# An RWKV attention and mixture-of-experts layer on one core: the first block in halves, products in front of three waits, two of the last rows ahead of the branch, one more bank at the end

## The chip, the cores and the metric

The kernel runs on 1 core of a Trainium2 chip. A core has a tensor engine (PE, with its weight loads shown apart as PEld), VectorE (DVE), ScalarE (ACT), GpSimd (POOL) and SyncE (SP), each with an instruction queue of its own that runs in order, and 16 DMA engines that all queues share. Matmul results land in PSUM, which has 8 banks of 128 x 512 float32 words. The metric is the device time of one execution in microseconds (us). Times below are us unless another unit is given.

## The reference

With x of shape (1, 2048, 512), all in float32:

```python
xn = layernorm(x)                                    # over the 512 columns, no weights
# attention: RWKV
r, v, k = split(xn @ W_rvk.T, 3)
# per column c, over the tokens t, with w = -exp(time_decay), u = time_first:
#   y  = (exp(o - no) * p + exp(u + kt - no) * vt) / (exp(o - no) * q + exp(u + kt - no))
#   o, p, q  <-  the running maximum and the two sums scaled to it
attn = (sigmoid(r) * y) @ W_out.T
# experts: 12, of which 8 are real and 4 pass x through; top 2 by softmax + bias
probs = softmax(xn @ classifier_w.T);  idx = top_k(probs + bias, 2);  rw = probs[idx] * 1.5
ffn = sum over the chosen real experts of rw * (silu(xn @ gate_e.T) * (xn @ up_e.T)) @ down_e.T
    + xn * (sum of rw over the chosen pass-through experts)
return x + attn + ffn
```

## The kernel before, in words

The 2048 tokens are four blocks b of 512, and a block is four rows j (row i = 4b + j) of 128 tokens. Everything is written in one hand-set order (`manual_schedule`): each engine runs its instructions in the order in which the Python code issues them.

**Head.** `load_x` and `load_w` put the loads on SP's queue. `norm(b)` (L207) takes the mean and variance of the block's four rows on DVE, then one chain for all four: sd on ACT (L218), seven small DVE instructions to rstd and shift, and the scaling of the rows, on DVE for even j (L232) and on ACT for odd j (L234). `turn_block(b)` (L237) transposes the block on PE, 4 columns c of 4 pieces, into four PSUM banks, each copied out by ACT (L246). The loop at L520 norms the next block while it turns this one, with classifier matmuls (`logits`, `add_quarters`, into the tile pl) and first products in between.

**Products.** `all_products` (L415) is a generator over all matmuls of k, v and r, 176 steps of two matmuls of 512 columns in four-byte floats (PE records each as two passes). k and v of a pair of blocks are made with seven products instead of eight (p1 to p7). Several share a bank: p6 writes a bank py, DVE adds it away; p7 adds into the same bank, DVE adds again (L368); p4 adds into it, DVE adds again (L385). So p7's first matmul waits for p6's add, and p4's first matmul for p7's add. Likewise p3 follows p5 in a bank pz. `fill(n)` issues the next n steps.

**Routing.** From pl, DVE chooses the two experts of each token (L547 to L648), and sorts tokens into 25 tiles of 128 places by expert: for m = 0 and 1 it makes the matrices lowhot and tok (L674 to L692), and PE multiplies them into pi (L695). Between the two, PE gets `fill(5)` (L698).

**Main part.** Sixteen scans (one for each block b and column c, `scan`, L460) run on DVE and ACT in five stages S1 to S5: S1 scans the running maximum, S2 takes exponentials on ACT, S3 scans the two sums, S4 forms the denominator and numerator, S5 divides (a reciprocal of 3.3 us) into yT. Twenty-five expert tiles run beside them. `first_half(i)` (L850) multiplies the tile with its experts' gate and up weights (`up`, L795, four matmuls into pg), applies the activation and asks for the weights of tile i + 2; `second_half(i)` (L866) packs the next tiles (`unite(i + 1)` makes xgT on ACT, L783; `flip(i + 2)`) and finishes tile i - 2 (`finish`, L833: the down product po, yo on ACT, and a scatter by POOL that adds it to the output in DRAM).

A plan sets the order: `plan(at, what)` puts a piece of work at a place in a table that is then sorted by that place. The product steps that are left stand at 0, `one`, 2 `one`, ..., the stages of the scans at fixed places, and the halves of tile i at `4 + spread * i` and `4 + spread * (i + 0.6)`. With 57 of the 176 steps issued before the table, 119 are left, and `one` is (259.86 - 8) / 151 = 1.668 and `spread` is (259.86 - 12) / 25 = 9.914:

```python
    total = (len(left) + CC * len(ROWS)) * ONE + TILES * 5.2
    one = (total - 8) / (len(left) + CC * len(ROWS))
    spread = (total - 12) / TILES
```

**Tail.** Rows of blocks 0 and 1 are multiplied with W_out during the main part (`attention_row`, L973). The rows of block 2 come after the table (`attention`, L905, in turn with the last stages of the last scan), each added to xn times its pass-through weight on DVE (L934). Then a branch (L1038) skips a loop that would run if the tokens needed more than 25 tiles; here it is never entered. After it, SP reads the output rows of block 3 back (`read_out`, which must wait for the last scatter), DVE adds the pass-through part (L901), POOL adds eight finished rows to the output in DRAM (`add_row`, L967, accumulating DMAs), and the four rows of block 3 are multiplied, added (L930) and written (L931), the last one in two halves in one bank.

PSUM is four pools of two banks: mm, gu, o and tr. A new tile takes the bank of its pool that was given back first, and its first writer waits until that bank's last reader is done.

Of the kernel before, what the change touches and what calls it, by code (L numbers as in the profile page):

```python
# [26 lines left out]
F32 = mybir.dt.float32  # L27
# [8 lines left out]
P = 128  # L36
T = 2048
C = 512
CC = C // P
TB = 512  # L40
NTB = T // TB
NJ = TB // P
# [9 lines left out]
TILES = 25  # L52
# [7 lines left out]
def layer(ctx: ExitStack, tc: tile.TileContext, x, w_rvk, w_out, decay, first, cls, ebias, gu, down, out):  # L60
    nc = tc.nc
# [6 lines left out]
    place = pool("place", 1)  # L68
# [6 lines left out]
    small = pool("small", 2)  # L75
# [128 lines left out]
    xnT = {}  # L204
    pl = ps_o.tile([P, NT, ET], F32, tag="o", name="pl")

    def norm(b):  # L207
        js = slice(b * NJ, (b + 1) * NJ)
        for j in range(NJ):
            i = b * NJ + j  # L210
            st = small.tile([P, 6], F32, tag="st", name=f"st{i}")
            nc.vector.bn_stats(st, xt[i])  # L212
            nc.vector.bn_aggr(mv[:, i, :], st)
        var = mv[:, js, 1]
        ve = small.tile([P, NJ], F32, tag="ve", name=f"ve{b}")
        nc.vector.tensor_scalar_add(ve, var, EPS)
        sd = small.tile([P, NJ], F32, tag="sd", name=f"sd{b}")
        nc.scalar.activation(sd, var, AF.Sqrt, bias=eps_sb[:, 0:1])  # L218
        r0 = small.tile([P, NJ], F32, tag="r0", name=f"r0{b}")
        nc.vector.reciprocal(r0, sd)  # L220

        sq = small.tile([P, NJ], F32, tag="sq", name=f"sq{b}")
        nc.vector.tensor_mul(sq, r0, r0)
        nc.vector.tensor_mul(sq, sq, ve)
        nc.vector.tensor_scalar(sq, sq, -0.5, 1.5, ALU.mult, ALU.add)
        nc.vector.tensor_mul(rstd[:, js], r0, sq)
        nc.vector.scalar_tensor_tensor(shift[:, js], mv[:, js, 0], -1.0, rstd[:, js], ALU.mult, ALU.mult)
        for j in range(NJ):
            i = b * NJ + j
            t, r = xt[i], rstd[:, i : i + 1]  # L230
            if j % 2 == 0:
                nc.vector.tensor_scalar(t, t, mv[:, i, 0:1], r, ALU.subtract, ALU.mult)  # L232
            else:
                nc.scalar.activation(t, t, AF.Identity, bias=shift[:, i : i + 1], scale=r)  # L234
        store_xn(b)

    def turn_block(b):  # L237
        xnT[b] = place.tile([P, CC, TB], F32, tag=f"s{2 + b}", name=f"xnT{b}")
        for c in range(CC):
            if c % 2 == 0:  # L240
                pt = ps_tr.tile([P, TB], F32, tag="tr", name=f"pt{b}_{c}")
            else:
                pt = ps_gu.tile([P, TB], F32, tag="gu", name=f"pt{b}_{c}")
            for j in range(NJ):
                nc.tensor.transpose(pt[:, j * P : (j + 1) * P], xt[b * NJ + j][:, c * P : (c + 1) * P], ident)
            nc.scalar.copy(xnT[b][:, c, :], pt)  # L246

    lgs = {}

# [205 lines left out]
    def fill(n):  # L455
        for _ in range(n):
            next(products)
        done[0] += n
# [52 lines left out]
    def whole(gen):  # L511
        for _ in gen:
            pass
# [1 line left out]

    manual = ExitStack()
    manual.enter_context(tc.manual_schedule())
    norm(0)
    turn_block(0)
    for b in range(NTB):  # L520
        if b + 1 < NTB:
            norm(b + 1)
# [149 lines left out]
    for m in range(2):  # L672
        ks = slice(m * NT, (m + 1) * NT)
        nc.vector.tensor_tensor(  # L674
            lowhot[:, ks, :],
            lane.unsqueeze(1).to_broadcast([P, NT, P]),
            low[:, m].unsqueeze(2).to_broadcast([P, NT, P]),
            ALU.is_equal,
        )
        nc.vector.tensor_tensor(  # L680
            hh,
            tiles128.unsqueeze(1).to_broadcast([P, NT, MAX_TILES]),
            high_b[:, m].unsqueeze(2).to_broadcast([P, NT, MAX_TILES]),
            ALU.is_equal,
        )
        tok = place.tile([P, NT, NV, MAX_TILES], BF16, tag=f"s{7 + m}", name=f"tok{m}")
        nc.vector.tensor_tensor(  # L687
            tok,
            hh.unsqueeze(2).to_broadcast([P, NT, NV, MAX_TILES]),
            vals[:, m].unsqueeze(3).to_broadcast([P, NT, NV, MAX_TILES]),  # L690
            ALU.mult,
        )  # L692
        for j in range(NT):
            k = m * NT + j
            nc.tensor.matmul(pi, lowhot[:, k, :], tok[:, j], start=(k == 0), stop=(k == NK - 1))  # L695
        if m == 0:
            which_i = place_tiles()
            fill(5)  # L698
    nc.vector.tensor_scalar_mul(wdec, wdec, -1.0)
    cfac = const.tile([P, CC], F32, tag="cfac", name="cfac")  # L700
    nc.vector.tensor_add(cfac, first_sb, wdec)
# [192 lines left out]
    def read_out(b):  # L894

        t = place.tile([P, NJ, C], F32, tag="s0", name=f"orows{b}")
        for j in range(NJ):
# [4 lines left out]
                orows[i], xrows[i], zw[:, i : i + 1], orows[i], ALU.mult, ALU.add  # L902
            )

    def attention(b, js=range(NJ)):  # L905

        for j in js:
            i = b * NJ + j
            if b < NTB - 2:
                po = ps_tr.tile([P, C], F32, tag="tr", name=f"pw{i}")  # L910
            elif j >= 2 if i in orows else j % 2 == 1:
                po = ps_mm.tile([P, C], F32, tag="mm", name=f"pw{i}")
            else:
                po = ps_o.tile([P, C], F32, tag="o", name=f"pw{i}")

            halves = 2 if i == NT - 1 else 1
            n = C // halves
            for h in range(halves):
                hs = slice(h * n, (h + 1) * n)
                for c in range(CC):  # L920
                    nc.tensor.matmul(  # L921
                        po[:, hs],
                        yT[b][:, j, c, :],
                        wout_sb[:, c, hs],
                        start=(c == 0),
                        stop=(c == CC - 1),
                    )
                    yield
                if i in orows:
                    nc.vector.tensor_add(orows[i][:, hs], orows[i][:, hs], po[:, hs])  # L930
                    nc.sync.dma_start(out[i * P : (i + 1) * P, hs], orows[i][:, hs])  # L931
            if i in orows:
                continue
            nc.vector.scalar_tensor_tensor(xrows[i], xrows[i], zw[:, i : i + 1], po, ALU.mult, ALU.add)  # L934

# [57 lines left out]
    def plan(at, what, *args):  # L993
        table.append((at, iter([(what, *args)]) if args else what))
# [108 lines left out]
```

## Time and profile before

| What | us |
|---|---|
| Time, median of 3 runs | 379.12 (378.87 to 379.74) |
| The profiled execution, time | 379.29 |
| The profiled execution, span | 377.5 |
| PE busy | 358.2 |
| DVE busy | 308.9 |
| ACT busy | 161.5 |
| POOL busy | 91.4 |
| First matmul starts | 10.37 |
| Last matmul ends | 374.15 |
| DMA moved | 88.80 MB, mean 235 GB/s |

A line of a timeline starts with the start and the duration of a group of instructions, then engine, source line, operation, tiles written <- tiles read and their shapes; brackets at the end give how long the engine stood idle before it and what ended that. A line of the waits reads: engine, tile, line <- who was waited for: us in total, times, longest. A line for a stretch gives its start and end, its length, and then the busy us (and number of instructions) of PE, PEld, DVE, ACT and POOL, the granted clock of PE, the busy share of the DMA engines and their GB/s. The busy share of the DMA engines can pass 1, since a packet's time holds time that it waits.

### The profile page before, as it was taken

To read this page: it belongs to the slowest core of one execution; us is meant where nothing else is said; L and a number is where in the kernel's file an instruction comes from. 1 tells how busy PE (TensorE), PEld (TensorE's weight loads), DVE (VectorE), ACT (ScalarE), POOL (GpSimd) and SP (SyncE) were. 2 spreads that over 40 slices of the span, in tenths; PEclk is the share of its full clock that TensorE was granted. 3 is DMA by queue.
4 is the path that set the end of the run, shared out by engine and by line. 5 is a ranking of instruction groups with operands and counts; after the bars stand their busy time and mean duration, and the time that the engine had idled before them with its cause. 6 is when DMAs were issued, how large, how long until landed. Compare 5 with 4: busy or idle time off the path is not lost.

```text
span 377.5 us, 3504 instructions
## 1 busy us (share of the span) xinstructions
PE 358.2 (95%) x970; PEld 164.9 (44%) x970; DVE 308.9 (82%) x450; ACT 161.5 (43%) x274; POOL 91.4 (24%) x118
## 2 busy tenths in 40 slices
PE   0899998999999999999999999999999999999995
PEld 0565444543444444444444444444444444444343
DVE  4879899989997997987987779597769786959951
ACT  1677311232653554554556453636354555423000
POOL 5000300210203233322232224133144321102450
PEclk9999999999999999999999999999999999999999
DMA  7998944643657898889898998999999999767497
GB/s 268 399 356 322 334 141 162 227 91 132 177 126 220 257 264 250 251 230 260 220 262 237 272 265 222 271 233 319 258 280 277 290 264 248 195 188 166 93 191 191
DMA packets 63029, 88.80 MB, mean 235 GB/s; under 512 B 42208, under 2 KB 42592, under 8 KB 59232
## 3 DMA queue, kind: packets, MB, share of 16 engines
q1 hardware_dynamic: 55472, 67.85, 61.5%
q0 software_dynamic: 7536, 20.71, 23.5%
q8 instruction: 8, 0.13, 0.1%
q14 instruction: 13, 0.11, 0.1%
HBM read 63.78 MB, written 19.40 MB: 220 GB/s over the span
## 4 chain that ended last, share of the span: by engine, by line
PE 73%; DVE 17%; DMA 5%; ACT 2%; issue 2%; SPq 0%; DVEq 0%
PE pg L795 22%; PE po L836 10%; PE pr L408 9%; PE py L325 9%; PE pw L973 7%; PE pz L325 6%; PE px L325 4%; PE pw L921 4%; DMA x<-in_x_dram 3%; DVE den L505 3%; DMA wrvk<-in_w_rvk_dram 2%; DVE tok L687 2%; DVE sums L490 1%; DVE obv L477 1%; DVE st L212 1%
## 5 line engine op out<-in xcount | busy, mean ns | idle before, releaser
L795 PE MATMUL pg<-gw,xgT 128*128 128x512 f32 x200 | 90.2, 593 | 1.5 <-ACT xgT L783 1.5
L841 POOL DMA_INDIRECT out_dram<-yo,to_i x25 | 45.7, 1826 | 165.0 <-ACT yo L840 114.5
L408 PE MATMUL pr<-xnT,wrvk 128*128 128x512 f32 x128 | 60.6, 593 | 0.0
L795 PEld LDWEIGHTS pg<-gw,xgT 128*128 128x128 f32 x200 | 37.8, 190 | 49.3 <-issue 45.7
L505 DVE RECIPROCAL den<-den 128x512 f32<-128x512 f32 x16 | 53.5, 3345 | 0.0
L836 PE MATMUL po<-dw,actT 128*128 128x512 f32 x100 | 46.9, 593 | 0.5 <-ACT actT L814 0.5
L803 ACT ACTIVATE th<-pg 128x256 f32<-128x256 f32 x25 | 9.6, 384 | 85.0 <-PE pg L795 85.0
L733 POOL DMA_INDIRECT xg<-xs,token_i x25 | 27.0, 1080 | 61.9 <-ACT xp L775 28.3
L408 PEld LDWEIGHTS pr<-xnT,wrvk 128*128 128x128 f32 x128 | 24.1, 190 | 29.2 <-issue 29.2
L804 DVE SCALAR_TENSOR_TENSOR th<-th,pg 128x256 f32<-128x256 f32 x25 | 10.5, 419 | 32.1 <-ACT th L803 32.0
L325 PE MATMUL px<-xnT,wrvk 128*128 128x512 f32 x64 | 32.3, 604 | 0.0
L325 PE MATMUL py<-t,wrvk 128*128 128x512 f32 x64 | 30.7, 594 | 0.0
L783 ACT COPY xgT<-xq 128x1024 uint16<-128x1024 uint16 x25 | 28.9, 1156 | 3.9 <-DMA xq<-xp 3.8
L921 PE MATMUL pw<-wout_sb,yT 128*128 128x512 f32 (+1 forms) x72 | 28.2, 548 | 2.0 <-DVE xrows L934 1.5
L973 PE MATMUL pw<-wout_sb,yT 128*128 128x512 f32 x64 | 30.1, 592 | 0.0
L836 PEld LDWEIGHTS po<-dw,actT 128*128 128x128 f32 x100 | 18.9, 190 | 24.2 <-issue 22.7
L775 ACT COPY xp<-xg 128x1024 uint16<-128x1024 uint16 x25 | 26.1, 1044 | 5.6 <-DMA xq<-xp 4.5
L840 ACT ACTIVATE yo<-po,wplace 128x512 f32<-128x512 f32 x25 | 17.2, 686 | 23.2 <-PE po L836 23.0
L490 DVE TENSOR_TENSOR_SCAN sums<-obv,state,a 128x512 f32<-128x512 f32 x16 | 20.5, 1282 | 4.1 <-ACT obv L483 4.0
L492 DVE TENSOR_TENSOR_SCAN sums<-obv,state,a 128x512 f32<-128x512 f32 x16 | 20.5, 1284 | 0.6
L921 PEld LDWEIGHTS pw<-wout_sb,yT 128*128 128x128 f32 x72 | 13.5, 190 | 17.0 <-issue 13.4
L477 DVE TENSOR_TENSOR_SCAN obv<-wdec,state,k 128x512 f32<-128x512 f32 x16 | 20.5, 1280 | 0.0
(171 smaller groups left out, 459.0 us busy)
## 6 DMA issues: line engine op xcount, KB each, us to landing
gw<-in_gu_dram SPq DMA_DIRECT2D x25, 1024.0 KB, 5.5
dw<-in_down_dram SPq DMA_DIRECT2D x25, 512.0 KB, 5.9
x<-in_x_dram SPq DMA_DIRECT2D x16, 256.0 KB, 5.3
xs<-x SPq DMA_DIRECT2D x16, 256.0 KB, 4.9
wrvk<-in_w_rvk_dram SPq DMA_DIRECT2D x3, 1024.0 KB, 7.2
xrow<-xs SPq DMA_DIRECT2D x8, 256.0 KB, 7.0
xrows<-xs SPq DMA_DIRECT2D x8, 256.0 KB, 5.2
wout_sb<-in_w_out_dram SPq DMA_DIRECT2D x1, 1024.0 KB, 10.6
```

The source lines that it names most:

```text
L325: nc.tensor.matmul(ps, a[:, k, c * P : (c + 1) * P], x[:, k], start=(start and k == 0), stop=(k == 1), skip_group_check=True,)
L408: nc.tensor.matmul(ps, wrvk_sb[0][:, k, c * P : (c + 1) * P], xnT[b][:, k, :], start=(k == 0), stop=(k == CC - 1))
L477: nc.vector.tensor_tensor_scan(o2, w.to_broadcast([P, TB]), k, s[:, 0:1], ALU.add, ALU.max)
L505: nc.vector.reciprocal(den, den)
L733: nc.gpsimd.indirect_dma_start(out=xg, out_offset=None, in_=xs, in_offset=bass.IndirectOffsetOnAxis(ap=token[:, i : i + 1], axis=0),)
L775: nc.scalar.copy(xp, st[i]["xg"].bitcast(U16).rearrange("p (c h) -> p h c", h=2))
L783: nc.scalar.copy(xgT.bitcast(U16).rearrange("p c (t h) -> p c t h", h=2), st[i]["xq"].rearrange("p (h c) t -> p c t h", h=2),)
L795: nc.tensor.matmul(pg, st[i]["xgT"][:, c, :], st[i]["w"][:, c, :], start=(c == 0), stop=(c == CC - 1))
L836: nc.tensor.matmul(po, st[i]["actT"][:, c, :], st[i]["d"][:, c, :], start=(c == 0), stop=(c == IC - 1))
L841: nc.gpsimd.indirect_dma_start(out=out, out_offset=bass.IndirectOffsetOnAxis(ap=to[:, i : i + 1], axis=0), in_=yo, in_offset=None, compute ...
L921: nc.tensor.matmul(po[:, hs], yT[b][:, j, c, :], wout_sb[:, c, hs], start=(c == 0), stop=(c == CC - 1),)
L973: nc.tensor.matmul(po, yT[b][:, j, c, :], wout_sb[:, c, :], start=(c == 0), stop=(c == CC - 1))
```

## The change

Block 0 is normalised and turned in two halves of two rows: `norm` and `turn_block` take a `part`, and the copies out of PSUM, the stores of xn and the tile xnT come with the second half. `fill(5)` between the two products of the routing becomes `fill(6)`, so that 58 steps are issued before the table and 118 are left. `first_half(1)` stands two places later in the plan. The first matmul of the first row of block 2 is put into the plan right ahead of `finish` of the last tile. The rows of blocks 2 and 3 take their banks from the pools o, tr, mm and o in pairs, and the second half of the last row takes a bank of tr. Rows 12 and 13 are multiplied ahead of the branch; their sums and stores follow behind it (`add_rows`), as those of rows 14 and 15 do.

```diff
-    def norm(b):
-        js = slice(b * NJ, (b + 1) * NJ)
-        for j in range(NJ):
+    def norm(b, part=range(NJ)):
+        n = len(part)
+        js = slice(b * NJ + part[0], b * NJ + part[0] + n)
+        for j in part:
...
-        store_xn(b)
-
-    def turn_block(b):
-        xnT[b] = place.tile([P, CC, TB], F32, tag=f"s{2 + b}", name=f"xnT{b}")
+        if part[-1] == NJ - 1:
+            store_xn(b)
+
+    pts = {}
+
+    def turn_block(b, part=range(NJ)):
         for c in range(CC):
-            if c % 2 == 0:
+            if part[0] > 0:
+                pt = pts[c]
+            elif c % 2 == 0:
                 pt = ps_tr.tile([P, TB], F32, tag="tr", name=f"pt{b}_{c}")
             else:
                 pt = ps_gu.tile([P, TB], F32, tag="gu", name=f"pt{b}_{c}")
-            for j in range(NJ):
+            pts[c] = pt
+            for j in part:
                 nc.tensor.transpose(pt[:, j * P : (j + 1) * P], xt[b * NJ + j][:, c * P : (c + 1) * P], ident)
-            nc.scalar.copy(xnT[b][:, c, :], pt)
+            if part[-1] == NJ - 1:
+                if c == 0:
+                    xnT[b] = place.tile([P, CC, TB], F32, tag=f"s{2 + b}", name=f"xnT{b}")
+                nc.scalar.copy(xnT[b][:, c, :], pt)
...
-    norm(0)
-    turn_block(0)
+
+    for part in (range(0, NJ // 2), range(NJ // 2, NJ)):
+        norm(0, part)
+        turn_block(0, part)
...
-            fill(5)
+            fill(6)
...
+    whole_rows = []
+
+    def add_rows():
+
+        for i, hs, po in whole_rows:
+            nc.vector.tensor_add(orows[i][:, hs], orows[i][:, hs], po[:, hs])
+            nc.sync.dma_start(out[i * P : (i + 1) * P, hs], orows[i][:, hs])
+        whole_rows.clear()
+
     def attention(b, js=range(NJ)):
-
         for j in js:
             i = b * NJ + j
-            if b < NTB - 2:
-                po = ps_tr.tile([P, C], F32, tag="tr", name=f"pw{i}")
-            elif j >= 2 if i in orows else j % 2 == 1:
-                po = ps_mm.tile([P, C], F32, tag="mm", name=f"pw{i}")
-            else:
-                po = ps_o.tile([P, C], F32, tag="o", name=f"pw{i}")
+
+            pool_, tag = ((ps_o, "o"), (ps_tr, "tr"), (ps_mm, "mm"), (ps_o, "o"))[(i - (NTB - 2) * NJ) // 2]
+            po = pool_.tile([P, C], F32, tag=tag, name=f"pw{i}")
...
+                if h == 1:
+                    po = ps_tr.tile([P, C], F32, tag="tr", name=f"pw{i}_{h}")
...
-                if i in orows:
-                    nc.vector.tensor_add(orows[i][:, hs], orows[i][:, hs], po[:, hs])
-                    nc.sync.dma_start(out[i * P : (i + 1) * P, hs], orows[i][:, hs])
-            if i in orows:
+                if b == NTB - 1:
+                    whole_rows.append((i, hs, po))
+                    yield
+            if b == NTB - 1:
                 continue
...
-        plan(4 + spread * i, first_half, i, TILES)
+
+        plan(4 + spread * i + (2 if i == 1 else 0), first_half, i, TILES)
         plan(4 + spread * (i + 0.6), second_half, i, TILES)
...
+    third = [attention(NTB - 2, [j]) for j in range(NJ)]
+    plan(6.9 + spread * TILES, third[0])
...
     for j, stops in enumerate((1, 2, 0, 0)):
-        whole(attention(NTB - 2, [j]))
+        whole(third[j])
         for _ in range(stops):
             next(stages[-1])
+    whole(attention(NTB - 1, range(0, 2)))
...
-    whole(attention(NTB - 1))
+    add_rows()
+    for _ in attention(NTB - 1, range(2, NJ)):
+        add_rows()
```

More of the change, by code (lines that the diff above doesn't have):

```diff
@@ L214, in norm @@
         var = mv[:, js, 1]
-        ve = small.tile([P, NJ], F32, tag="ve", name=f"ve{b}")
+        ve = small.tile([P, NJ], F32, tag="ve", name=f"ve{b}_{part[0]}")[:, :n]
         nc.vector.tensor_scalar_add(ve, var, EPS)
-        sd = small.tile([P, NJ], F32, tag="sd", name=f"sd{b}")
+        sd = small.tile([P, NJ], F32, tag="sd", name=f"sd{b}_{part[0]}")[:, :n]
         nc.scalar.activation(sd, var, AF.Sqrt, bias=eps_sb[:, 0:1])
-        r0 = small.tile([P, NJ], F32, tag="r0", name=f"r0{b}")
+        r0 = small.tile([P, NJ], F32, tag="r0", name=f"r0{b}_{part[0]}")[:, :n]
         nc.vector.reciprocal(r0, sd)
-        sq = small.tile([P, NJ], F32, tag="sq", name=f"sq{b}")
+        sq = small.tile([P, NJ], F32, tag="sq", name=f"sq{b}_{part[0]}")[:, :n]
         nc.vector.tensor_mul(sq, r0, r0)
@@ L243, in turn_block @@
                 pt = ps_gu.tile([P, TB], F32, tag="gu", name=f"pt{b}_{c}")
-            for j in range(NJ):
+            pts[c] = pt
+            for j in part:
                 nc.tensor.transpose(pt[:, j * P : (j + 1) * P], xt[b * NJ + j][:, c * P : (c + 1) * P], ident)
-            nc.scalar.copy(xnT[b][:, c, :], pt)
+            if part[-1] == NJ - 1:
+                if c == 0:
+                    xnT[b] = place.tile([P, CC, TB], F32, tag=f"s{2 + b}", name=f"xnT{b}")
+                nc.scalar.copy(xnT[b][:, c, :], pt)
     lgs = {}
```

## The prediction

> **What bounds the kernel now.** I read the page first, then the waits of the tensor engine (PE), then the timeline at the three places where PE waits, and last the stretches of the end.
>
> The busy times and what PE waited for:
>
> ```profile
> PE 358.2 (95%) x970; PEld 164.9 (44%) x970; DVE 308.9 (82%) x450; ACT 161.5 (43%) x274; POOL 91.4 (24%) x118
> ```
> ```profile
> PE pt L245 <- DVE x L232: 10.4, 1, 10.4
> PE pg L795 <- ACT xgT L783: 1.5, 1, 1.5
> PE pw L921 <- DVE xrows L934: 1.5, 1, 1.5
> PE pi L695 <- DVE tok L687: 1.4, 1, 1.4
> PE po L836 <- ACT actT L814: 0.5, 1, 0.5
> PE pw L921 <- DVE orows L930: 0.5, 1, 0.5
> ...
> PEld py L325 <- DVE v L368: 1.2, 2, 0.9
> ```
>
> PE is the bound; its idle time lies in six places, and the change goes at each. The last line (all engines' waits) is the one to remember: a weight load that waited for VectorE (DVE) to read a product out of its bank.
>
> The head, in the timeline:
>
> ```profile
> 7.31 0.69 DVE L212 BATCH_NORM_STATS2 st<-x 128x6 f32<-128x512 f32 x1 [1.12 <-DMA x<-in_x_dram]
> 10.37 3.91 PE L245 MATMUL pt<-ident,x 128*128 128x128 f32 x16 [10.37 <-DVE x L232]
> 14.11 1.88 PE L325 MATMUL px<-xnT,wrvk 128*128 128x512 f32 x4
> 14.79 0.30 ACT L218 ACTIVATE sd<-mv,eps_sb 128x4 f32<-128x4 f32 x1
> 19.60 1.91 PE L245 MATMUL pt<-ident,x 128*128 128x128 f32 x16
> ```
>
> DVE sits idle for the fourth row of x while two rows could already be normalised. The middle, on DVE, PE and the weight loads, and one stretch of 21.9 us:
>
> ```profile
> 101.17 3.34 DVE L505 RECIPROCAL den<-den 128x512 f32<-128x512 f32 x1
> 105.16 0.68 DVE L368 TENSOR_TENSOR v<-v,py 128x512 f32<-128x512 f32 x1
> 108.41 0.68 DVE L368 TENSOR_TENSOR v<-v,py 128x512 f32<-128x512 f32 x1
> ```
> ```profile
> 103.81 3.60 PE L795 MATMUL pg<-gw,xgT 128*128 128x512 f32 x8
> 107.24 3.03 PE L325 MATMUL py<-t,wrvk 128*128 128x512 f32 x6
> ```
> ```profile
> 109.15 0.30 PEld L325 LDWEIGHTS py<-t,wrvk 128*128 128x128 f32 x2 [0.85 <-DVE v L368]
> ```
> ```profile
> 83.30:105.20 21.90, 20.36 (x48) 8.77 (x48) 21.61 (x26) 7.83 (x13) 2.66 (x2) 1.00 0.58 154
> ```
>
> In that stretch (PE, weight loads, DVE, ScalarE (ACT), POOL) DVE is busy 21.61 of 21.90: there DVE, not PE, has no slack. The end, with the DMA share and GB/s in the last columns:
>
> ```profile
> 364.00:369.00 5.00, 5.00 (x13) 2.19 (x12) 2.48 (x4) 0.00 (x0) 0.86 (x1) 1.00 1.12 204
> 369.00:374.00 5.00, 4.49 (x19) 3.05 (x17) 1.11 (x2) 0.00 (x0) 0.00 (x0) 1.00 1.08 276
> 374.00:375.00 1.00, 0.16 (x1) 0.00 (x0) 0.42 (x1) 0.00 (x0) 0.00 (x0) 1.00 0.27 89
> 375.00:376.10 1.10, 0.00 (x0) 0.00 (x0) 0.00 (x0) 0.00 (x0) 0.00 (x0) 1.00 0.39 134
> ```
>
> The DMA engines are full from 358 to 374 (eight accumulating rows of POOL's queue, then output rows) and only the last 2 us have room. The chain of waits names PE there; behind PE stands a second bound just as late.
>
> **Head: block 0 in halves.** The second row's statistics end at 5.09. What takes from 8.26 to 9.68 on DVE (variance to scaling, 1.42) now runs from 5.13, the first two rows are scaled by 7.1 (DVE) and 7.4 (ACT, 0.76). The seven extra small DVE instructions (0.16 to 0.18 each) fall where DVE waited for the fourth row. Rows three and four: statistics 7.0 to 8.7, scaled by 10.7 and 11.1, against 10.68 and 11.31 before; DVE starts block 1 at 10.7, as before (10.66). PE turns 8 of 16 pieces from 7.1 to 9, the other 8 from 11.1 at 0.2 us each, done near 12.6 instead of 14.1. ACT's four copies end near 13.7 instead of 14.9, so block 1's sd leaves at 14.0 (its variances are ready at 13.95) instead of 14.79: block 1 is scaled, and the copy of the first product behind it on ACT leaves, 0.8 earlier. PE needs that copy for p2 (weight load at 18.37, waiting for ACT v). So 1.5 on PE becomes about 0.85, and everything up to the routing (DVE reads pl at 37.84 after a wait of 0.32 for PE) moves by it. Ends: 1.0, set by ACT's copy; and a loss of 0.3 if the products from 12.6 run at half pace until 16.3.
>
> Why half pace: the transposes before 14.0 take 0.20 each (13 weight loads in 2.63), those at 19.6 take 0.12, and the four products at 14.11 come every 0.43, the full pace of the whole kernel. So PE sped up about 3.6 us after it began. I let it speed up at 14.0 again; four products from 12.65 are then done at 15.1, still ahead of ACT's copy at 17.6. [...]
>
> **Middle: fill(6), and first_half(1) two units later.** One product step (two matmuls at 0.43, 0.86) goes into the wait of 1.35 for tok; DVE sets the end of that wait, so what is saved is the 0.86 later. But every product now runs one place earlier against DVE's stages. Walking the queues with the rows' durations, from 66.27 - 0.85 = 65.42:
> - p7 of column 0 now meets the deferred adds and p4 of column 0 meets p7's add, both still on DVE: waits of 0.15 and 0.43. So DVE's add for p5 of column 1 (83.32, which waited 0.19 for PE) comes 0.86 - 0.58 = 0.28 earlier beside the 0.85.
> - The plan now puts seven product steps between tiles 0 and 1, not six. PE reaches tile 1 at 93.58 - 0.85 + 0.58 + 0.86 = 94.17; ACT's xgT, behind DVE's chain, is ready at 95.07 - 0.85 - 0.28 = 93.94. The wait of 1.54 is gone, with 0.2 to spare.
> - Next in line: p4 of column 2 adds into the bank that p7's add reads (DVE, 105.16). Before, the plan held it at 25.02, behind tile 2 (23.83): PE did 3.43 us of pg first. One slot is now (259.0 - 8)/150 = 1.673, p4 is slot 14 at 23.43, and tile 2 stands at 23.76: p4 goes in front. PE arrives at 94.17 + 3.43 + 4 x 0.86 = 101.0. DVE has the same 21.6 us of work before that add, so it ends at 105.84 - 0.85 - 0.28 = 104.7: a new wait of 3.7.
> - The old wait of 0.27 for the second such add (108.41; load at 109.15) goes.
>
> With first_half(1) go ACT's packing copy for tile 0, SyncE's load of tile 3's weights (5.5 to land, wanted some 15 later) and POOL's gather for tile 4 (4.5, likewise); I cost them at nothing for that cover, and at most at the 0.9 by which they leave later.
>
> Sum on PE up to the last tile, from which DVE's last chain hangs (it waited 4.18 for that tile): -0.85 - 0.86 - 1.54 - 0.27 + 0.58 + 3.7 = +0.76. Later waits I expect none: PE idled 0.03 us from 96 to 332, and xgT for tiles 3 and 4 is ready 4 us early. Bounds of the new wait: nothing, if DVE keeps up, and 4.3, if DVE gains only the 0.85 less 0.3.
>
> **End.** The row matmul in front of finish (0.86) covers the wait of 0.52 for actT; it changes POOL's scatters by nothing, since each waits some 5.6 for the one before (345.08, 350.65, then 356.23). The first products of row 12 and the bank wait (1.5, 0.5) go: the last yT ends at 358.64, and 13 row matmuls of 0.86 follow instead of 16 from 359.36. PE ends at 369.9 instead of 374.15: 4.3 earlier, beside the +0.76. A branch between rows 13 and 14 costs PE little: before, PE's semaphore write behind it followed its last matmul by 0.04; at most the 1.5 that PE stood idle there, under the 4.3. DVE, four row sums held by reads that land until 363.8, adds rows 12 and 13 at 365.2, before 365.11 and 366.53; SyncE's five writes leave between 365.6 and 370.4 instead of 374.6. But they wait for DMA engines: a write issued at 365.82 took 6.6 to land, as accumulations filled them (204 GB/s alone). Bytes are the same, so only the idle part goes: 0.73 of 374 to 375 and 0.67 of 375 to 376.1, 1.4 in all. The last accumulation (issued 364.18, 10.6 to land) lands at 374.8 and the program ended 1.2 after its last landing: 1.5 is the most. I take 1.15, nearer to the idle rows, as the last packets spread unevenly; least 0.4, should the last half row (1.7 to land) still come alone.
>
> Sum: +0.76 - 1.15 = -0.4 on a span of 377.5; with 1.79 around it (379.29) 378.9, and with the median 0.17 lower, 378.7.
>
> **Rivals.**
> - The new wait at p4 is not there (DVE keeps up, or the order falls otherwise). For it: before, it cost 0.85 only. Against: the 21.61 of 21.90. Then -3.5 + 0.58 = -2.9, and -1.15: 375.1.
> - Slower: PE stays at half pace from 12.65 to 16.3. Place: the four products and the eight logits matmuls; price 1.8, so that block 1's transposes come at 19.9 instead of 18.75. It decides from about 15.5 on. Then the head loses 0.3, and +1.9 - 1.15 = +0.75: 379.9 to 380.3. For it: PE now pauses from 9 to 10.7. Against: 14.11 came at full pace after 3.7 us.
> - The earlier output rows slow the accumulations and the end gains nothing: +0.76, 379.9. Against: mixed, the engines moved 276 GB/s, alone 204.
> - No change at all to be seen is part of the main case: under 0.2% (0.76 us, about what a measurement of this kernel can tell).
>
> **How the numbers follow.** Main case 0.48, 378.7 with an own range of 377.4 to 379.9; no new wait 0.18; half pace 0.17; no gain at the end 0.10; the rest 0.07. Faster by over 0.2%: a third of the main case, the first rival, some of the rest: 0.37. Slower: a fifth of the main case, half of each of the two others and some rest: 0.26. Same 0.37. The range leaves out half of the first rival and the far end of the slow ones: 375.2 to 380.3.
>
> **What would show it.** Products from about 12.6 and block 1 turned near 18.8; the wait for tok 0.5, none for xgT; a wait of 3 to 4 us of PE for DVE's L368 add near 101 to 105; no waits at actT, xrows, orows; PE done 4 us before the end, and DMA engines full until the last microsecond. Wrong if PE passes p4 without waiting (375), or if products near 13 come every 0.86 for over 3 us.

## The result, and the profile after

| What | before | after |
|---|---|---|
| Median of all executions, us | 379.13 (378.50 to 383.66, 20) | 383.50 (379.75 to 388.69, 20) |
| Ratio, 95% interval | | 1.0085 (1.0060 to 1.0111) |
| Profiled execution, time / span, us | 379.29 / 377.5 | 380.86 / 379.0 |
| Start of the last tile's second half of pg | 331.78 | 333.14 |
| Last matmul ends | 374.15 | 372.55 |
| Last scatter of POOL leaves | 350.65 | 352.08 |

The change makes the kernel slower by 0.85%, 3.2 us. The ratio leaves out four executions of the changed kernel that took over 1.5% more than its fastest (386.02 to 388.69); with them the medians lie 1.15%, 4.4 us, apart. I had forecast 378.7, and 380.3 at the most. The profiled execution is among the quickest of the changed kernel and shows only 1.5 us of the loss in its span; the other half has to be looked for in the executions that it does not show.

The busy times and the waits of the tensor engine (PE), from the page and the view of waits, of the changed kernel (waited for, us in total, times, longest):

```profile
PE 359.4 (95%) x970; PEld 165.2 (44%) x970; DVE 309.9 (82%) x457; ACT 162.0 (43%) x275; POOL 90.9 (24%) x118
```
```profile
PE pt L251 <- DVE x L233: 8.6, 2, 7.2
PE py L334 <- DVE v L377: 3.7, 2, 3.6
PE pi L706 <- DVE tok L698: 0.5, 1, 0.5
```

Of the six idle places before, those at xgT, actT, xrows and orows are gone, tok has shrunk from 1.4 to 0.5, and one of 3.6 us has come: PE waits for a VectorE (DVE) add that reads the bank which p4 of column 2 writes next.

The head, in the timeline (start, duration, then the group):

```profile
7.17 2.06 PE L251 MATMUL pt<-ident,x 128*128 128x128 f32 x8 [7.17 <-DVE x L233]
10.67 2.15 PE L251 MATMUL pt<-ident,x 128*128 128x128 f32 x8 [1.44 <-DVE x L233]
12.60 2.88 PE L334 MATMUL px<-xnT,wrvk 128*128 128x512 f32 x4
...
19.09 1.91 PE L251 MATMUL pt<-ident,x 128*128 128x128 f32 x16
```

The first products start 1.5 us earlier (12.60 for 14.11) but take 2.88 instead of 1.88, as PE reaches its full pace only at 14.61. Block 1 is turned 0.51 earlier.

The middle, on PE and then on DVE:

```profile
94.42 3.70 PE L806 MATMUL pg<-gw,xgT 128*128 128x512 f32 x8
97.96 3.60 PE L334 MATMUL py<-t,wrvk 128*128 128x512 f32 x8
105.13 1.13 PE L334 MATMUL py<-t,wrvk 128*128 128x512 f32 x2 [3.57 <-DVE v L377]
106.09 3.60 PE L806 MATMUL pg<-gw,xgT 128*128 128x512 f32 x8
109.52 2.74 PE L334 MATMUL py<-t,wrvk 128*128 128x512 f32 x6
```
```profile
100.40 3.35 DVE L514 RECIPROCAL den<-den 128x512 f32<-128x512 f32 x1
103.78 0.69 DVE L515 TENSOR_TENSOR yT<-num,den 128x512 f32<-128x512 f32 x1
104.39 1.28 DVE L377 TENSOR_TENSOR v<-v,py 128x512 f32<-128x512 f32 x2
```

p4 stands in front of tile 2, and PE has nothing else that it may do in the meantime. Tile 2, which started at 103.81 before, starts at 106.09.

The end, in stretches (busy time of PE, weight loads, DVE, ScalarE (ACT) and POOL, then the granted clock, the DMA share and GB/s):

```profile
366.00:371.00 5.00, 5.00 (x18) 3.09 (x17) 2.86 (x6) 0.00 (x0) 0.69 (x1) 1.00 1.14 205
371.00:376.00 5.00, 1.56 (x8) 1.02 (x6) 0.71 (x2) 0.00 (x0) 0.00 (x0) 1.00 0.99 276
376.00:377.00 1.00, 0.00 (x0) 0.00 (x0) 0.00 (x0) 0.00 (x0) 0.00 (x0) 0.71 0.19 61
```

PE ends 1.6 us earlier than before, and the program 1.5 later: 6.4 us pass between PE's last matmul and the end, where before it was 3.4. The accumulating rows go at 205 GB/s with the DMA share at 1.14, as before (204 at 1.12).

### The profile page after: what moved, and what is told of

It reads as the page before. It is cut to its first block, busy times and chain, and to the rows that moved or that the text cites. A ratio compares the mean times of both kernels' runs of the same rounds, so it can differ in the third digit from the quotient of the medians.

```text
span 379.0 us, 3515 instructions
## 1 busy us (share of the span) xinstructions
PE 359.4 (95%) x970; PEld 165.2 (44%) x970; DVE 309.9 (82%) x457; ACT 162.0 (43%) x275; POOL 90.9 (24%) x118
## 5 line engine op out<-in xcount | busy, mean ns | idle before, releaser
L939 PE MATMUL pw<-wout_sb,yT 128*128 128x512 f32 (+1 forms) x72 | 28.1, 546 | 0.1
L334 PEld LDWEIGHTS py<-t,wrvk 128*128 128x128 f32 x64 | 11.9, 190 | 20.0 <-issue 12.9
```

What stands on the lines that cost most here:

```text
L334: nc.tensor.matmul(ps, a[:, k, c * P : (c + 1) * P], x[:, k], start=(start and k == 0), stop=(k == 1), skip_group_check=True,)
L939: nc.tensor.matmul(po[:, hs], yT[b][:, j, c, :], wout_sb[:, c, hs], start=(c == 0), stop=(c == CC - 1),)
```

## The experiments

Three theories were put against each other. A: the pause of 3.57 us costs its length and, besides, the granted clock of PE, in most executions. B: the split of block 0 disturbs the clock. C: the end hangs on the DMA engines, so that what PE gives there is lost. The clock of each execution below is the mean granted clock over its span. Where PE ends well before the program, half pace in the last idle microseconds takes 0.002 to 0.005 off it at no cost (0.998 in the first profile with the head whole, 0.995 in that of the rows added early; in the changed kernel's first profile it begins at 376.42, 3.9 behind PE's last matmul, and the clock is 0.997), so that 0.995 to 0.998 can be an execution with no loss.

**Tile 2 ahead of p4 again.**

```diff
-        plan(4 + spread * i + (2 if i == 1 else 0), first_half, i, TILES)
+        plan(4 + spread * i + (2 if i == 1 else -0.5 if i == 2 else 0), first_half, i, TILES)
```

> The changed kernel, with the first half of tile 2 planned 0.5 units earlier (23.26), so that p4 of column 2 (23.43) stands behind it again, as in the kernel before; nothing else is different. Theory A (PE's pause of 3.57 us in front of that p4 is the loss, and it is also what lets PE's clock fall to half for some us in most executions): the wait at line 334 near 105 is gone, the last tile's matmuls end near 330.4 instead of 333.14, the granted clock is 0.997 or more in nearly every execution, and the median is near 377.5, 1.6 under the kernel before. Theory B (the split of block 0 disturbs the clock, the pause costs only itself): the wait is gone too, but most executions still show clocks of 0.98 to 0.99, and the median is near 380.5. Theory C (the end is bound by the DMA engines whatever PE does): PE ends some 9 us before the span does, and the median is no lower than 378.5.

Measured: 377.83, ratio 0.9945 (0.9911 to 0.9979), clocks 0.997 and above in 10 of 12, 0.995 in two. Of the pause 0.2 us is left. The waits and the head of its profiled execution:

```profile
PE pt L251 <- DVE x L233: 8.7, 2, 7.3
PE pi L706 <- DVE tok L698: 0.5, 1, 0.5
PE py L334 <- DVE v L377: 0.2, 1, 0.2
```
```profile
12.73 3.62 PE L334 MATMUL px<-xnT,wrvk 128*128 128x512 f32 x4
...
20.31 1.91 PE L251 MATMUL pt<-ident,x 128*128 128x128 f32 x16
```

One number in the plan turns a loss of 3.2 us into a gain of 2.1. Theory A holds. B falls as far as it needs the split alone, since the split is in here. But the head came out badly in this execution: PE got its full pace at 17.04, so the four products took 3.62 and block 1 was turned at 20.31, later than the 19.60 of the kernel before. That is the half pace that I had as a rival.

**Block 0 in one piece, the rest as changed.**

```diff
-    for part in (range(0, NJ // 2), range(NJ // 2, NJ)):
+    for part in (range(NJ),):
```

> The changed kernel with block 0 normalised and turned in one piece, as before; middle and end as changed. Theory A: the pause in front of p4 of column 2 stays at about 3.6 us, the clocks of the executions stay spread from 0.98 to 1.0, the work to the last tile ends 0.5 later (333.6 against 333.14), and the median is near 384. Theory B (the early transposes and the stop between the halves disturb the clock): every execution has a clock of 0.998 or more, and the median is near 381.2, which is the profiled 380.86 with the 0.5 of the head taken back.

Measured: 382.99, ratio 1.0096 (1.0064 to 1.0128), clocks from 0.987 to 0.998. The loss stays without the split. B falls.

**The split alone**, in the kernel before.

```diff
-    norm(0)
-    turn_block(0)
+    for part in (range(0, NJ // 2), range(NJ // 2, NJ)):
+        norm(0, part)
+        turn_block(0, part)
```

> The kernel before, with block 0 in halves and nothing else. Block 1's transposes on PE come near 19.1 instead of 19.6. My prediction's step gave the head 0.85 and the trace of the changed kernel shows 0.50; how much of it reaches the last tile depends on DVE, which has no slack from 83 to 105: theory A: the median is between 378.4 and 379.2, with clocks as steady as those of the kernel before. Theory B: the clocks spread from 0.98 to 1.0, and the median is 381 to 382.

Measured: 379.55, ratio 1.0005 (0.9975 to 1.0035), clocks 0.998 to 1.0. The split doesn't harm the clock, and no gain shows, though the interval would hide one of 0.5. Why the earlier turn of block 1 (18.82 here, 19.60 before) is not seen in the median is told further down.

**The end alone**, in the kernel before (the banks and `add_rows` of the change are in as well and are not shown again).

```diff
+    third = [attention(NTB - 2, [j]) for j in range(NJ)]
+    plan(6.9 + spread * TILES, third[0])
...
+    whole(attention(NTB - 1, range(0, 2)))
...
-    whole(attention(NTB - 1))
+    add_rows()
+    for _ in attention(NTB - 1, range(2, NJ)):
+        add_rows()
```

> The kernel before, with the end of the change alone: the first row matmul ahead of the last finish, two rows of block 3 ahead of the branch, one bank more. My prediction's step: PE ends near 370 instead of 374.15, the whole program 1.15 earlier, median 378.0. Theory C (accumulations and output rows share the DMA engines and these are full either way, so that what PE gives is lost): PE ends near 370, the last landing stays within 0.4 of 376.0, and the median is 378.9 to 379.5.

Measured: 378.75, ratio 0.9985 (0.9963 to 1.0008). The interval leaves both open; the profile tells them apart: PE ended at 371.24 (374.15 before), the last output packet at 374.97 (376.00), the span was 376.5. That speaks against C, which had it within 0.4 of 376.00: the end gained 1.0 of my 1.15 in that execution, 0.3 of it already at the last scatter (350.36 for 350.65). The last stretch, which idled before at shares of 0.27 and 0.39, is half full:

```profile
368.50:373.50 5.00, 2.73 (x13) 2.08 (x11) 0.85 (x3) 0.00 (x0) 0.00 (x0) 1.00 1.09 270
373.50:375.00 1.50, 0.00 (x0) 0.00 (x0) 0.00 (x0) 0.00 (x0) 0.00 (x0) 1.00 0.57 205
```

**The middle alone**, in the kernel before.

```diff
-            fill(5)
+            fill(6)
...
-        plan(4 + spread * i, first_half, i, TILES)
+        plan(4 + spread * i + (2 if i == 1 else 0), first_half, i, TILES)
```

> The kernel before, with fill(6) and the later first_half(1) alone. Theory A: TensorE pauses 3.6 us in front of p4 of column 2; the last tile's second half of pg starts at 333.6 (331.78 before); clocks spread from 0.985 to 1.0; the median is 382.5 to 384, all of the loss of the changed kernel. If the loss needed the three parts together (the head's stop or the earlier output rows adding to it): the median is 381.0 or less, the 1.8 of the wait alone, with clocks of 0.999 to 1.0.

Measured: 383.61, ratio 1.0118 (1.0072 to 1.0164), and this time the profiled execution has what the medians had only hinted at:

```profile
105.20 1.33 PE L334 MATMUL py<-t,wrvk 128*128 128x512 f32 x2 [3.57 <-DVE v L377]
106.33 5.13 PE L806 MATMUL pg<-gw,xgT 128*128 128x512 f32 x8
111.30 2.74 PE L334 MATMUL py<-t,wrvk 128*128 128x512 f32 x6
```

The eight matmuls of tile 2 behind the pause take 5.13 instead of 3.60. The trace's clock record has half pace from 105.99 for 3.41 us. From p4's start to the work behind tile 2 it is 6.10 us, where the changed kernel's first profile had 4.39 (105.13 to 109.52): 1.71 lost beside the pause. All of the loss is in the middle.

**The pause by itself, in the old order.** A reciprocal whose result the next add overwrites holds DVE up, in the kernel before, ahead of an add for which a weight load of PE already waited 0.85.

```diff
-        nc.vector.tensor_add(kvr_tile("v", b + 1, c), kvr[b, c, "v"], ps)
+        v = kvr_tile("v", b + 1, c)
+        if (b, c) == (0, 3):
+            for _ in range(1):
+                nc.vector.reciprocal(v[:, :420], kvr[b, c, "v"][:, :420])
+        nc.vector.tensor_add(v, kvr[b, c, "v"], ps)
```

> The kernel before, with one reciprocal of 420 columns (2.74 us by the 3.34 of 512 columns) put on VectorE ahead of its add at line 368 for column 3, whose result is overwritten by that add. TensorE's wait of 0.85 for that add near 109 becomes one pause of about 3.6 us, as long as the pause of the changed kernel, in the old order of the work. Theory A (a pause of this length also drops the granted clock in most executions): clocks of 0.985 to 0.997 in most executions, where those of the kernel before have 0.999 to 1.0, and a median of 383 to 385, 1 to 3 above what the pause alone costs. Theory D (a pause costs its own length and the spread of the changed kernel's executions has another origin): clocks of 0.999 to 1.0 and a median of 381.8 to 382.4, the 2.74 above the kernel before.

> The same with two reciprocals of 460 columns, 6.0 us: TensorE pauses for 6.9 us in one piece near 109. Theory A: every execution, the profiled one too, has a stretch at half clock that begins in or right after the pause, with matmuls of 128x512 every 0.85 us instead of 0.43; clock 0.985 to 0.995, median 386.5 to 389.5. Theory D: the clock record stays at full from 14 to the end, clocks 0.999 to 1.0, median 385 to 385.7.

> The kernel before with two reciprocals of 262 columns (3.42 us) in place of the 2.74 of the run with 420 columns, whose pause came out at 2.91 and left the clock of 6 of its 8 executions at 0.999 to 1.0. The pause is now 3.6, that of the changed kernel, in the old order of the work. [...] Theory E (the changed order brought the drop, not the length): clocks of 0.999 to 1.0 in at least three of four executions, median 382.6 to 383.6.

The kernels with one reciprocal of 420 columns, two of 262 and two of 460, one line or two of each after the pause:

```profile
112.29 1.12 PE L325 MATMUL py<-t,wrvk 128*128 128x512 f32 x2 [2.91 <-DVE v L372]
113.25 1.88 PE L840 MATMUL po<-dw,actT 128*128 128x512 f32 x4
```
```profile
113.56 1.12 PE L325 MATMUL py<-t,wrvk 128*128 128x512 f32 x2 [3.75 <-DVE v L372]
114.52 3.32 PE L840 MATMUL po<-dw,actT 128*128 128x512 f32 x4
```
```profile
115.12 2.08 PE L325 MATMUL py<-t,wrvk 128*128 128x512 f32 x2 [6.22 <-DVE v L372]
116.98 3.55 PE L840 MATMUL po<-dw,actT 128*128 128x512 f32 x4
```

| Pause of PE's matmuls, us | Executions below 0.998 | Half pace in the profile | Median, us | Ratio (95%) |
|---|---|---|---|---|
| 1.54 at most (the kernel before, at xgT) | 4 of 94 | none | 379.13 to 379.76 | |
| 2.91 | 2 of 8 | none | 383.36 | 1.0100 (1.0063 to 1.0136) |
| 3.75 | 5 of 6 | 3.41 us | 384.05 | 1.0121 (1.0088 to 1.0153) |
| 6.22 | 6 of 6 | 6.83 us | 388.65 | 1.0276 (1.0220 to 1.0331) |

The first came out 0.7 shorter than I had reckoned, and for the clock as theory D had it: a pause of 2.9 us left it whole in 6 of 8. At 3.75 theory A is right and E falls: the length does it, not the order. With 6 to 8 executions each, the table doesn't say where between 2.91 and 3.75 the chance turns. The median of the first is in A's range (383 to 385), not D's: 3.8 above the kernel before for a delay of 2.74. Its interval reaches down to 2.4. In its profile, 3.7 longer than that of the kernel before, 0.3 lies in the head, 2.9 at the pause and 0.5 behind the last tile; whether the other executions share this is not shown.

**The changed kernel again**, twice as it is, and once more with block 0 in one piece. Where the first of the three expectations speaks of windows, it means stretches of 3.41 us at half pace, as the middle alone had one from 105.99.

> The changed kernel as it is, for a second profile. Theory A: clocks near 0.997 (none), 0.992 (one window) and 0.988 (two) as in the executions so far, median 383 to 384; should the profiled execution have a drop, its granted clock goes to half at the end of, or within 2 us after, the pause in front of p4 of column 2, for 3.4 or 6.8 us, and nowhere else before TensorE's last matmul.

> The changed kernel a third time, one look. In its two profiles the end of the program followed the last scatter by 26.9 and 27.2 us, in four other kernels with the same end by 26.0 to 26.1. Theory C1 (how fast POOL's accumulations go differs from execution to execution): 26.0 to 27.2, anywhere. Theory C2 (the changed kernel's own order makes them slow): 26.9 or more again.

> The changed kernel with block 0 in one piece again, one look: its end followed the last scatter by 26.0. Theory C1: 26.0 to 27.2, anywhere. Theory C2: 26.2 or less again. By theory A a drop of the clock, if this execution has one, lies right behind the pause in front of p4 of column 2 and is 3.4 or 6.8 us long.

The second profile had no drop (382.61 in the median, for 383 to 384 expected; ratio 1.0085 once more, 1.0053 to 1.0117). The third, an execution of 387.30, has:

```profile
106.06 2.08 PE L334 MATMUL py<-t,wrvk 128*128 128x512 f32 x2 [3.58 <-DVE v L377]
107.93 5.67 PE L806 MATMUL pg<-gw,xgT 128*128 128x512 f32 x8
113.43 2.74 PE L334 MATMUL py<-t,wrvk 128*128 128x512 f32 x6
```
```profile
105.20:112.10 6.90, 6.04 (x7) 2.52 (x8) 4.02 (x7) 0.00 (x0) 0.00 (x0) 0.51 0.27 68
```

The granted clock (0.51, third column from the right) is at half for 6.83 us, from 105.25, still inside the pause. From p4 to the work behind tile 2 it takes 7.37 instead of 4.39: 2.98 lost, and a later tile waits 1.3 for its xgT besides. The kernel with the head whole, profiled again, had 3.41 us at half from 106.02 and lost 1.70 (105.01 to 111.10).

Sorted by their granted clock, the 31 executions of the changed kernel are:

| Granted clock | Executions | Median, us |
|---|---|---|
| 0.994 and more | 14 | 381.44 |
| 0.990 to 0.993 | 9 | 383.45 |
| 0.989 and less | 8 | 386.2 |

Between the groups lie 2.0 and 2.7 us; the traces give 1.7 for a stretch of 3.41 us at half pace and 3.0 for one of 6.83. So, by their clocks, more than half of the executions lose 1.7 or 3 us that the first profile, one of the other 14, doesn't show.

As to the end, the program ended 28.1 us after the last scatter in the third profile of the changed kernel (26.9 and 27.2 in the first two), and 28.3 where the head was whole, which had 26.0 the first time. Both lie outside C1's range, and the second rules out C2: the end varies from execution to execution of one kernel, by more than C1 allowed and by more than it has to give. It is the new end that varies: the six profiles with the end of the kernel before have 26.8 to 27.1. In the stretch of the third profile in which it all comes to a stop, the DMA share is a tenth:

```profile
376.00:380.00 4.00, 2.04 (x10) 1.45 (x8) 0.84 (x2) 0.00 (x0) 0.00 (x0) 1.00 1.09 270
380.00:382.00 2.00, 0.00 (x0) 0.00 (x0) 0.00 (x0) 0.00 (x0) 0.00 (x0) 0.93 0.73 233
382.00:384.00 2.00, 0.00 (x0) 0.00 (x0) 0.00 (x0) 0.00 (x0) 0.00 (x0) 0.50 0.09 26
```

For some 1.6 us (the last output packet ended at 383.62) fewer than two of sixteen DMA engines, in the mean, still had packets.

**What the head is worth.** Tile 2 first and block 0 in one piece, both against the changed kernel:

```diff
-    for part in (range(0, NJ // 2), range(NJ // 2, NJ)):
+    for part in (range(NJ),):
...
-        plan(4 + spread * i + (2 if i == 1 else 0), first_half, i, TILES)
+        plan(4 + spread * i + (2 if i == 1 else -0.5 if i == 2 else 0), first_half, i, TILES)
```

> The changed kernel with tile 2 ahead of p4 and with block 0 in one piece: what is left is fill(6), the later first_half(1) and the end. By the profile of the changed kernel the split was worth 0.5 (block 1 turned at 19.09 instead of 19.60); in the profile of the run with the split and tile 2 first TensorE ran at half pace until 17.04 and block 1 was turned at 20.31. Theory H1 (the split gains 0.5 in the middle of the executions): median 0.3 to 0.6 above the same kernel with the split, 378.2 to 378.5. Theory H2 (with the split the moment of the speed-up falls anywhere from 13.7 to 17.0, and what it gains it loses as often): the median is 376.8 to 377.8, not above the kernel with the split, and the executions lie closer together.

Measured: 377.06, ratio 0.9940 (0.9911 to 0.9970). H2 holds in the median: not above the kernel with the split (377.83). The executions lie no closer together, 375.34 to 380.48 against 376.00 to 381.08. The profiles show two reasons. One is the moment of full pace: with the split, block 1 was turned at 18.82, 19.09, 19.11, 19.72, 20.02 and 20.31 as PE sped up at 13.70, 14.61, 14.55, 15.78, 16.51 and 17.04; without it, in eleven profiles, at 18.62 to 20.32 as it sped up between 12.87 and 15.83. The middle of both is near 19.4. The other is that the wait which the split was to fill is not always there. In the profile of the kernel before, DVE waited 1.12 for the fourth row of x; in the one with tile 2 first and the head whole the row was there:

```profile
5.38 0.69 DVE L213 BATCH_NORM_STATS2 st<-x 128x6 f32<-128x512 f32 x1 [0.37 <-DMA x<-in_x_dram]
6.11 0.18 DVE L214 BATCH_NORM_AGGREGATE mv<-st 128x2 f32<-128x6 f32 x1
6.21 0.66 DVE L213 BATCH_NORM_STATS2 st<-x 128x6 f32<-128x512 f32 x1
```

There PE turned its first piece at 9.22, not 10.37. I had taken one execution's transfer for the kernel's.

**The rows of block 1 added early**, in pairs behind the third and fourth of them, with tile 2 first; once with block 0 whole and once in halves.

```diff
-            late.append(i)
-        if b == 0 and j % 2:
-            add_row(i - 1)
-            add_row(i)
+        if b == 0 and j % 2 or b == 1 and j >= 2:
+            k = i - 1 if b == 0 else 2 * i - 8
+            add_row(k)
+            add_row(k + 1)
```

> The changed kernel with tile 2 ahead of p4 and block 0 in one piece, and the four rows of block 1 added to the output in pairs by POOL as soon as two of them are done (behind the third and the fourth), not after the branch: four accumulations of 256 KB leave the end, some 5 us of the DMA engines at 205 KB per us. Theory C (accumulations and output rows together set the end in that kernel): the last landing follows TensorE's last matmul (near 369) by some 3 us, the span is 372.5 to 373.5 and the median 375 to 376, 1 to 2 below the kernel with the same head and middle. If TensorE and not the DMA engines set the end: the median stays at 377. If the pairs hold up POOL's scatters behind them: the last scatter leaves later than 348.5 and the median is 377.5 or more.

> The same with block 0 in halves. Theory H2 (the split gains as often as it loses): within 0.6 of the kernel with block 0 in one piece. Theory H1 (the split gains 0.5): 0.3 to 0.7 below it.

Measured: 381.56, ratio 1.0022 (0.9995 to 1.0049), one execution of 552.72 at a clock of 0.663 aside, which stays unexplained; and 383.14, ratio 1.0073 (1.0043 to 1.0103). The third of my outcomes: the pairs held POOL's scatters up. PE itself waited 2.51 us near 345 for ACT's yo (2.86 with halves), a wait that is not there without the pairs.

```profile
314.77 1.88 POOL L985 DMA_DIRECT2D out_dram<-yT  x2 [6.11 <-DMA out_dram<-yo,to_i]
324.65 1.62 POOL L852 DMA_INDIRECT out_dram<-yo,to_i  x1 [8.01 <-DMA out_dram<-yT]
```

The scatter that left at 317.20 without them leaves at 324.65, and the last at 359.14 for 348.50. All the same it fits C's account of the end: the program ended 21.1 after the last scatter (380.2), and 21.7 with halves, against 26.0 with four accumulations more (374.5). Four rows of 256 KB are 1.05 MB, which take 5.1 us at 205 GB/s. With halves it was 1.6 slower in the median than without, outside what H1 and H2 had forecast.

**The last scatter moved**, with tile 2 first and block 0 in one piece. The finish of the last tile but two comes before the other work behind the last tile's products, and its packing copy before them.

```diff
+        if i == n - 1:
+            unite_act(i - 2)
...
-        if i > 1:
+        if i == n - 1:
+            finish(i - 2)
+        elif i > 1:
             unite_act(i - 2)
...
-        if i > 1:
+        if 1 < i < n - 1:
             finish(i - 2)
```

> The changed kernel with tile 2 ahead of p4 and block 0 in one piece, and now the finish of the last tile but two moved ahead in the order: its actT is packed on ScalarE at the start of the last tile's first half and its four matmuls follow the last tile's gate and up products at once (near 331.5 instead of 334.0). Its scatter leaves POOL near 334.2 instead of 337.0, and the two scatters behind it, each of which waits 5.6 to 5.8 for the one before, come the same 2.8 earlier. Theory C (the end of the changed kernel is the last scatter plus some 26.1 of accumulations and output rows): last scatter near 345.7 instead of 348.5, span 372.2 to 373.0 until TensorE's last matmul (369.1) plus 3.4 binds again, median 374.8 to 376.2. If TensorE's end sets it alone: span 374.5 as before, median 377.

Measured: 376.97, ratio 0.9928 (0.9914 to 0.9943); span 373.6. Its scatters:

```profile
326.06 1.55 POOL L852 DMA_INDIRECT out_dram<-yo,to_i  x1 [8.65 <-ACT yo L851]
335.56 2.05 POOL L852 DMA_INDIRECT out_dram<-yo,to_i  x1 [7.95 <-DMA out_dram<-yo,to_i]
341.49 1.55 POOL L852 DMA_INDIRECT out_dram<-yo,to_i  x1 [3.88 <-DMA out_dram<-yo,to_i]
347.05 1.55 POOL L852 DMA_INDIRECT out_dram<-yo,to_i  x1 [4.01 <-ACT a L491]
```

The moved scatter then waited for the one before it to land, and left only 1.46 earlier, as did the last (347.05 for 348.50). The span fell by 0.9, and 0.44 of that is the head (last tile at 329.22 for 329.66). So it doesn't tell C from PE: 0.5 of 1.46 came out. It is the fastest kernel of the study, 0.72% under the kernel before, though its interval overlaps with that of the two others with tile 2 first.

## Why the prediction was wrong

- **New wait at p4: right in place and length, wrong in price.** I had 3.7, it was 3.57, in the order that I worked out (p4 at 23.43 ahead of tile 2 at 23.76), and the small waits ahead of it were there (0.15 at 73.72). The failed step is that the sum booked it at 3.7 and put the clock behind it at nothing, without a reason. It costs its length and, in 17 of 31 executions by their clocks, 1.7 or 3.0 us of half pace behind it. I had weighed the clock only at the head. In the profiles half pace lasted 3.41 us (behind the pause of 3.57 in the middle alone and with the head whole again, and behind that of 3.75) or 6.83 us (with 3.58 in the changed kernel's third profile, and with 6.22). By the clocks it came in 17 of 31 executions with the pause of 3.57, in 5 of 6 with 3.75 and in 2 of 8 with 2.91.
- **Head: 0.85 forecast, 0.51 in the first profile, none to be seen in the medians.** The step "I let it speed up at 14.0 again" failed: it was 14.61, and in other executions up to 17.04. The rival with half pace, which I gave 0.17, is not a rival but the far end of what the same kernel does from one execution to the next. And the wait for the fourth row, from which the whole part was reckoned, is in some executions only.
- **Waits for tok and xgT: right.** 0.5 is left of 1.35 at tok, and the 1.54 at xgT is gone.
- **The sum to the last tile: +0.76 forecast, +1.36 measured.** 0.35 of the 0.6 between is the head's; the rest I have not traced to a term.
- **End: 1.15 forecast, 1.0 in the end alone, none in the first profile.** All three waits of PE went, as forecast. PE ended 2.9 earlier beside the shift (374.15 to 371.24 with the end alone), not 4.3: no more than the waits of 0.52, 1.52 and 0.51 and a little could go, since it was busy otherwise. It made no difference, as the DMA engines set the end in both reckonings. From the last scatter to the end it was 26.9 before, and with the new end 26.0 to 26.2 in four profiles and 26.9 to 28.3 in four others (26.5 with the scatter moved). The rival "the end gains nothing" took place in the profile that stands beside the forecast, and not by the mechanism that I gave: the accumulations went at the same 205 GB/s.
- **Range.** Its upper end, 380.3, took in one mishap of 1.5 us. The bounds of the new wait went from nothing to its own 4.3; the clock behind it, the one unknown that adds to it, was not in it.

For the profile without a drop the terms are +1.36 to the last tile and +0.1 at the end, 1.5 on the span. A drop in more than half of the executions, by their clocks, brings 1.7 to 3.0 more, and the median lies 3.2 to 4.4 above the kernel before. The group without a drop is at 381.44 in the median, and the kernel before has executions of 381 to 382 at a clock of 1.0 too; what these have in common, beside the head and the end varying, stays open.

## What to carry to other kernels

Here a pause of the tensor engine had two prices: its length, and half pace behind it in some of the executions (2 of 8 after 2.91 us, 17 of 31 after 3.57). Short waits (1.54, 0.85 and 0.27) taken out at the cost of one of 3.6 were a bad trade even though the sums were near each other, and a plan that moves work past waits should be searched for its longest pause, and not for the total alone. When a profile agrees with the forecast and the median doesn't, the other executions have something that this one hasn't: here the mean granted clock of each said what it was, and further profiles of the same order showed where.

## What the runs showed that I had not expected

- The place and the length of half pace differ from execution to execution. Behind pauses of 3.57 that ended at 105.20 (the middle alone) and 105.01 (the head whole again) it began at 105.99 and 106.02 and lasted 3.41 us; in the third profile of the changed kernel it began at 105.25, inside a pause that ended at 106.06, and lasted 6.83. The first full pace fell between 12.87 and 17.04, 3.2 to 6.1 us after PE's first transpose where these ran without a stop.
- One and the same pause drops the clock in one execution and not in the next. Of the six profiles with a pause of 3.57 to 3.58, three have a drop behind it (the middle alone, the changed kernel's third, the head whole again) and three have none; the first of the changed kernel kept full pace for 361.81 us, from 14.61 on, with the pause in it. What decides it is not shown.
- A pause of 2.91 us left the clock whole in 6 of 8 executions, one of 3.75 in 1 of 6.
- The same end took 26.0 to 28.3 us after the last scatter. In the two slowest the DMA share sank to 0.22 (head whole again, 377.0 to 379.8) and 0.09 (third profile of the changed kernel, 382.0 to 384.0) near the end; in two of the quickest it was 0.59 (tile 2 first, 372.0 to 374.5) and 0.57 (the end alone, 373.5 to 375.0). Why the last packets come so thinly in some executions stays open.
- Two accumulating rows put into POOL's queue between scatters delayed the next scatter by 7.5 us (317.20 to 324.65), since the pair waited for the scatter before it to land (6.11) and the next scatter for the pair (8.01).
